# A two-pass state-space layer and a ConvLSTM on one core: PSUM banks, scan buffers and the slots of the preparation rearranged

## The chip, the cores and the metric

The kernel runs on one core of one Trainium2 chip. The metric is device time in microseconds (us), the median of several runs; lower is better.

## The reference, cut to what matters

The input has 64 channels, 256 time steps and 128 frequencies, in f32. Layer 0 runs a bidirectional Mamba block along time (128 sequences of length 256), then another along frequency (256 sequences of length 128), each with a forward and a backward direction. Layer 1 is a ConvLSTM, which the change doesn't touch. What counts here is the Mamba block:

```python
def _mamba(u, p):
    xz = jnp.einsum('nld,ed->nle', u, p['in_proj_w'])
    x, z = jnp.split(xz, 2, axis=-1)                      # 128 channels each
    x = silu(depthwise causal conv of 4 taps over x)
    dt, Bm, Cm = jnp.split(jnp.einsum('nld,ed->nle', x, p['x_proj_w']), [4, 20], axis=-1)
    dt = softplus(jnp.einsum('nlr,dr->nld', dt, p['dt_proj_w']) + p['dt_proj_b'])
    A = -jnp.exp(p['A_log'])                              # 128 channels x 16 states
    def step(h, inp):
        dt_t, B_t, C_t, x_t = inp
        h = jnp.exp(dt_t[:, :, None] * A) * h + dt_t[:, :, None] * B_t[:, None, :] * x_t[:, :, None]
        return (h, jnp.einsum('nds,ns->nd', h, C_t))
    y = scan(step) + x * p['Dp']
    return jnp.einsum('nld,od->nlo', y * silu(z), p['out_proj_w'])
```

The block normalises its input first (root mean square over channels) and adds the input at the end. So each pass has, for each direction, 128 channels x 16 states x 32768 positions of a first-order recurrence.

## The kernel before

`Stage` holds one pass; `tile_kernel` runs it twice, with L = 256 (time) and L = 128 (frequency). A pass goes over 64 chunks (NCH) of 512 positions (2 sequences of 256, or 4 of 128). A chunk has 16 steps S: 8 for each direction d. `where(S)` (L565) names a step by chunk, direction, q (which half of the states) and b (which 32 channels). One step handles 32 channels x 8 states x 512 positions, laid out as 128 partitions (4 groups j of states by 32 channels) x 1024 (two states g by 512 positions).

The work of one step:

- `inputs` (L570): 32 matmuls on PE put dt * x * B into a tile bx of two PSUM banks. The left operand is dtxT, dt * x transposed, 64 rows by 32 columns; the right one is D, a diagonal that carries B, 64 rows by 128 columns (L579).
- `decays` (L588): ACT computes exp(A * dt) into dA, a ring of 4 tiles, from rep, which is dt spread over the partitions (L599). The first column of each sequence is copied from zeros (L596), for the first four steps of each eight only, since the ring keeps it.
- `recur` (L601): one scan on VectorE, h <- dA, bx (L607), into one of 7 tiles h.
- `outputs` (L610): POOL multiplies h by C, spread over the partitions (L613).
- `add_up` (L615), once in four steps: 8 matmuls fold states and channels into y in PSUM (L622).

`skip` (L634), `gate` (L638), `close` (L642 on, po, L680) and `keep` (L686, L694) finish a direction or a chunk. D is built by `diagonal` on VectorE: mask, a tile in SBUF, times bt, which is B transposed and stands in a PSUM bank of its own (L471). It has 64 columns for each of two states; so a direction needs two of them (q = 0 and 1), each built in two halves: 8 instructions of 128 x 1024 a chunk.

The preparation of a chunk is done ahead, during the chunk before it. `run` (L711) writes the order out by hand, for every engine at once, step by step: scan S, gate, outputs of S - 1, add_up, inputs of S + 2, decays of S + 2 (two at once in the step of the silus, none in the next), and then whatever the table HEAD (L73) names for this slot. A slot is a step of the chunk before, from -12 (two chunks before) to 25. HEAD names load, squares, means, rms and normalise (slots -12 to -5), the projections of x and z (-2, -1, 0), the silus (6), the step sizes dt (6 and 7), dt_away (8 and 14: the step sizes written to a DRAM tensor named there, four copies), project_bc (8: B and C, and C written to a DRAM tensor named away), times_x (dtx, on POOL), turn (10 and 18: dtxT and bt by transposes on PE), spread_dt (rep read back from there) and spread_c (C read back from away). All DMAs are issued by SP, in this order. [...]

[...] two tiles bx of two banks (four banks), two banks `mm` that all projections, transposes and means take in turn, one for y, one for bt. A matmul into an `mm` bank waits until ACT has read what was there.

Of the kernel before, what the change touches and what calls it, by code (L numbers as in the profile page):

```python
# [29 lines left out]
F32 = mybir.dt.float32  # L30
BF16 = mybir.dt.bfloat16
AF = mybir.ActivationFunctionType
# [28 lines left out]
NRING = 4  # L61
NREP = 3
RESPOND = 12
NH = 7
LAG = 2
# [7 lines left out]
HEAD = (  # L73
    (-12, "load"),
    (-7.5, "squares"),
    (-6, "means"),
    (-6, "rms"),
    (-5, "normalise"),
    (-2, "project_x", 0),
    (-1, "project_z"),  # L80
    (0, "project_x", 1),
    (6, "silus"),
    (6, "step_sizes"),
    (7, "softplus"),
    (8, "dt_away", 0),
    (8, "project_bc", 0, 1),
    (8.5, "times_x", 0),
    (9.5, "spread_dt", 0, 0),
    (10, "turn", 0),
    (10, "spread_c", 0, 0),  # L90
    (11, "diagonal", 0, 0, 0),
    (12, "spread_dt", 0, 1),
    (12.5, "times_x", 1),
    (13, "diagonal", 0, 0, 1),
    (13.5, "spread_c", 0, 1),
    (14, "dt_away", 1),
    (15, "diagonal", 0, 1, 0),
    (17, "diagonal", 0, 1, 1),
    (17, "spread_dt", 1, 0),
    (17.5, "spread_c", 1, 0),  # L100
    (18, "turn", 1),
    (19, "diagonal", 1, 0, 0),
    (20, "spread_dt", 1, 1),
    (21, "diagonal", 1, 0, 1),
    (21.5, "spread_c", 1, 1),
    (23, "diagonal", 1, 1, 0),
    (25, "diagonal", 1, 1, 1),
)
SECOND = tuple(x for x in HEAD if x[0] >= 12 and x[1] != "dt_away")

# [114 lines left out]
class Stage:  # L225
# [8 lines left out]
    def __init__(self, ctx, m, stage, L, X, src, moments, gates):  # L234
# [5 lines left out]
        self.time = stage == 0  # L240
        n = f"s{stage}_"
        self.io = ctx.enter_context(tc.tile_pool(name=n + "io", bufs=1))
        self.wk = ctx.enter_context(tc.tile_pool(name=n + "wk", bufs=1))
        self.st = ctx.enter_context(tc.tile_pool(name=n + "st", bufs=NH))
        self.dram = ctx.enter_context(tc.tile_pool(name=n + "dram", bufs=3, space=bass.MemoryType.DRAM))
        fixed = ctx.enter_context(tc.tile_pool(name=n + "fixed", bufs=1))
        self.ps_mm = ctx.enter_context(tc.tile_pool(name=n + "mm", bufs=2, space=PSUM))
        self.ps_bx = ctx.enter_context(tc.tile_pool(name=n + "bx", bufs=2, space=PSUM))
        self.ps_y = ctx.enter_context(tc.tile_pool(name=n + "y", bufs=1, space=PSUM))
        self.ps_bt = ctx.enter_context(tc.tile_pool(name=n + "bt", bufs=1, space=PSUM))  # L250
# [4 lines left out]
        self.zeros = fixed.tile([P, 2, 2, self.nseq // 2, 1], F32, name="zeros", tag="zeros")  # L255
        nc.gpsimd.memset(self.zeros, 0.0)
        self.dA = []
        for k in range(NRING):
            self.dA.append(fixed.tile([P, 2, 2, self.nseq // 2, L], F32, name=f"dA{k}", tag=f"dA{k}"))
# [43 lines left out]
    def normalise(self, ch):  # L303
        nc, n, L, unp = self.nc, self.nseq // 2, self.L, self.unp
        xn = self.io.tile([P, n, L], F32, name="xn", tag="xn")
        nc.gpsimd.tensor_mul(xn, self.at["u", ch], self.rs)
# [24 lines left out]
    def gated(self, pz):  # L331
        for d in range(2):
            rows = slice(d * C, (d + 1) * C)
            self.nc.tensor.matmul(  # L334
                self.seqs(pz[d]),
                lhsT=self.m.Wz[self.stage][rows],
                rhs=self.unp[rows, :, 3 + d : 3 + d + self.L],
                start=True,
                stop=True,
            )  # L340

    def project_x(self, ch, d):
        i = 2 * self.stage + d
        px = self.mm("px")
        xs = self.wk.tile([P, NTOK], F32, name="xs", tag="xs", bufs=4)
        self.shifted(px, i)
        self.nc.scalar.activation(xs, px, AF.Identity, bias=self.m.cb[:, i : i + 1])  # L347
        self.at["xs", ch, d] = xs

    def project_z(self, ch):  # L350
        pz = [self.mm("pz") for _ in range(2)]
        self.gated(pz)
        for d in range(2):
            zs = self.wk.tile([P, NTOK], F32, name="zs", tag="zs", bufs=5)
            self.nc.scalar.copy(zs, pz[d])  # L355
            self.at["zs", ch, d] = zs
# [15 lines left out]
    def step_sizes(self, ch):  # L372
        for d in range(2):
            self.step_size(ch, d)

# [7 lines left out]
    def softplus(self, ch):  # L383
        self.nc.scalar.preload_act_table_set(SOFTPLUS)
        for d in range(2):
            self.soft(ch, d)
# [907 lines left out]
```

## Time and profile before

| what | us |
|---|---|
| median of 3 runs (7128.19 to 7153.43) | 7144.68 |
| the profiled execution | 7169.17 |
| its span | 7167.4 |
| busy: PE, VectorE (DVE), ACT, POOL | 5830.0, 6368.4, 4829.9, 5567.1 |
| VectorE idle ahead of its scans, in all | 497.4 |
| of that until PE's bx, until ACT's dA | 310.4, 157.8 |
| ACT idle until rep came by DMA | 163.7 |
| DMA: bytes moved, mean rate | 921.86 MB, 129 GB/s |

The profile is of one execution. A row of its groups gives line, engine, operation, output and inputs with their shapes, count, then the busy time in us and the mean of one in ns, then the time that the engine sat idle just before, and what ended that. In the timeline a row is one or several like instructions in order: start, duration, engine, line. PE's weight loads (PEld) run beside its matmuls. An f32 matmul shows as two records. Some 36 of 40 slices of the span belong to the two passes, the rest to the ConvLSTM.

### The profile page before, as it was taken

What the parts mean: (1) busy time and instruction counts of PE and PEld (TensorE: products, weight loads), DVE (VectorE), ACT (ScalarE), POOL (GpSimd) and SP (SyncE); (2) the same over time, 40 slices, a digit from 0 to 9 for tenths busy, and PEclk for the clock granted to TensorE, in tenths of its full rate; (3) what the DMA queues carried; (4) which work ended last, traced back from release to release, by engine and by line L of the source; (5) the groups of instructions that cost most, each with busy time, mean ns of one, the idle gap of its engine ahead of it and who ended that gap; (6) DMA issues with size and microseconds to landing.
All of it is one profiled execution on the core that took longest, in us unless ns stands there. A gap on an engine that the chain in (4) does not pass through costs nothing.

```text
span 7167.4 us, 327118 instructions
## 1 busy us (share of the span) xinstructions
PE 5830.0 (81%) x150024; PEld 3482.0 (49%) x150024; DVE 6368.4 (89%) x4166; ACT 4829.9 (67%) x8730; POOL 5567.1 (78%) x2898
## 2 busy tenths in 40 slices
PE   7878777777877787877888888787887878778998
PEld 4444444444444444444444444444444444447887
DVE  7999898889999999988988889999989899896887
ACT  6767676767767677767777677777767677763333
POOL 6888888778888888877887778888888788784554
PEclk9999999999999999999999899999999999999999
DMA  5555555555555555545555555555555555550000
GB/s 134 152 146 139 145 139 145 133 145 139 143 149 138 146 152 136 149 116 150 137 149 133 148 132 147 135 144 150 130 143 133 140 134 144 132 140 35 14 16 17
DMA packets 412666, 921.86 MB, mean 129 GB/s; under 512 B 52372, under 2 KB 142100, under 8 KB 411288
## 3 DMA queue, kind: packets, MB, share of 16 engines
q1 hardware_dynamic: 411288, 900.93, 48.8%
q8 instruction: 1177, 19.28, 1.1%
q14 instruction: 201, 1.65, 0.1%
HBM read 557.32 MB, written 310.38 MB: 121 GB/s over the span
## 4 chain that ended last, share of the span: by engine, by line
PE 25%; DVE 11%; ACT 8%; issue 6%; DMA 2%; POOL 2%; SPq 1%; DVEq 0%; POOLq 0%; ACTq 0%
DVE h L607 8%; PE bx L579 6%; PE cv L1048 6%; ACT dA L599 4%; PE y L622 3%; DVE D L471 2%; PE px L328 2%; PE px L329 1%; POOL h L613 1%; PE pv L370 1%; DMA unp<-xn 1%; PE pz L334 1%; PE pg L1104 1%; PE both L1160 1%; ACT L387 1%
## 5 line engine op out<-in xcount | busy, mean ns | idle before, releaser
L613 POOL TENSOR_TENSOR h<-h,C 128x1024 f32<-128x1024 f32 x2048 | 4826.7, 2374 | 974.8 <-DVE h L607 781.2
L607 DVE TENSOR_TENSOR_SCAN h<-dA,bx 128x1024 f32<-128x1024 f32 x2048 | 4618.0, 2276 | 497.4 <-PE bx L579 310.4
L579 PE MATMUL bx<-D,dtxT 64*32 64x128 f32 x131072 | 2509.0, 281 | 1180.5 <-DVE h L607 799.5
L579 PEld LDWEIGHTS bx<-D,dtxT 64*32 64x32 f32 x131072 | 1926.4, 108 | 2312.4 <-issue 1125.7
L599 ACT ACTIVATE dA<-rep,cols 128x510 f32<-128x510 f32 (+1 forms) x4096 | 2648.1, 710 | 171.2 <-DMA rep<-there 163.7
L471 DVE TENSOR_TENSOR D<-mask,bt 128x1024 f32<-128x1024 f32 x1026 | 1227.6, 1197 | 34.6 <-PE bt L458 34.0
L622 PE MATMUL y<-h,fold 128*32 128x512 f32 x8192 | 1106.4, 659 | 5.4 <-POOL h L613 5.4
L347 ACT ACTIVATE xs<-px,cols 128x512 f32<-128x512 f32 x252 | 173.4, 688 | 898.5 <-PE px L329 898.5
L622 PEld LDWEIGHTS y<-h,fold 128*32 128x32 f32 x8192 | 243.5, 117 | 612.8 <-issue 566.2
L407 POOL TENSOR_TENSOR dtx<-dt,xs 128x512 f32<-128x512 f32 x256 | 327.3, 1279 | 71.7 <-ACT dt L380 71.2
L460 ACT COPY dtxT<-pt 128x512 f32<-128x512 f32 x256 | 149.9, 585 | 300.6 <-PE pt L456 300.6
L328 PE MATMUL px<-unp,g 128*128 128x512 f32 x504 | 313.7, 706 | 46.5 <-DMA unp<-xn 46.3
L370 PE MATMUL pv<-xs,wdt 128*128 128x512 f32 x512 | 278.4, 669 | 34.0 <-ACT xs L364 31.8
L329 PE MATMUL px<-unp,g 128*128 128x512 f32 x504 | 277.3, 633 | 0.5 <-issue 0.5
L638 DVE TENSOR_TENSOR yz<-y,zs 128x512 f32<-128x512 f32 x256 | 172.7, 675 | 74.9 <-PE y L622 72.7
L355 ACT COPY zs<-pz 128x512 f32<-128x512 f32 x252 | 134.9, 586 | 154.5 <-PE pz L334 148.6
L1171 POOL TENSOR_TENSOR y<-v,X 128x512 f32<-128x512 f32 x32 | 40.6, 1269 | 231.2 <-DVE v L1169 231.2
L596 ACT COPY dA<-zeros 128x4 f32<-128x4 f32 (+1 forms) x1024 | 197.4, 193 | 5.4 <-DVE h L607 4.0
L634 ACT ACTIVATE y<-xs,cols 128x512 f32<-128x512 f32 x256 | 175.6, 686 | 9.5 <-DVE yz L638 9.5
L1120 ACT ACTIVATE a<-pg,cols,scale 128x488 f32<-128x488 f32 x128 | 86.5, 756 | 135.6 <-DVE pg L1118 135.6
L680 PE MATMUL po<-yz,w 128*64 128x256 f32 x1024 | 172.5, 400 | 0.9 <-ACT dA L599 0.9
L380 ACT ACTIVATE dt<-pv,cols 128x512 f32<-128x512 f32 x256 | 164.3, 684 | 12.7 <-issue 6.2
(190 smaller groups left out, 5195.8 us busy)
## 6 DMA issues: line engine op xcount, KB each, us to landing
there<-dt SPq DMA_DIRECT2D x1024, 256.0 KB
rep<-there SPq DMA_DIRECT2D x512, 512.0 KB
C<-away SPq DMA_DIRECT2D x512, 512.0 KB
away<-bc SPq DMA_DIRECT2D x1024, 32.0 KB
unp<-xn SPq DMA_DIRECT2D x504, 64.0 KB
u<-in_x SPq DMA_DIRECT2D x128, 64.0 KB
out<-y SPq DMA_DIRECT2D x32, 256.0 KB
w<-in_W_ih_f SPq DMA_DIRECT2D x10, 512.0 KB
```

The costliest lines, as they stand in the source:

```text
L328: nc.tensor.matmul(self.seqs(px), lhsT=m.G1[i], rhs=self.unp[:, :, first : first + L], start=True, stop=False)
L329: nc.tensor.matmul(self.seqs(px), lhsT=m.G2[i], rhs=self.unp[:, :, second : second + L], start=False, stop=True)
L370: self.nc.tensor.matmul(pv, lhsT=self.m.Wdt[i], rhs=self.at["xs", ch, d], start=True, stop=True)
L407: self.nc.gpsimd.tensor_mul(self.in_turns(dtx, own), self.in_turns(self.at["dt", ch, d], natural), self.in_turns(self.at["xs", ch, d], nat ...
L471: self.nc.vector.tensor_mul(D, self.m.mask.unsqueeze(1).unsqueeze(1).to_broadcast([P, n, 2, W]), b.unsqueeze(3).to_broadcast([P, n, 2, W]),)
L579: self.nc.tensor.matmul(bx[DB * j : DB * (j + 1), i, :, u], lhsT=dtxT[rows, u, DB * b : DB * (b + 1)], rhs=D[rows, u, j], start=True, stop ...
L596: nc.scalar.copy(dA[:, :, :, :, first : first + 1], self.zeros)
L599: nc.scalar.activation(dA[:, :, g, :, live], rep[:, :, :, live], AF.Exp, scale=m.A[:, k, n : n + 1])
L607: self.nc.vector.tensor_tensor_scan(h[:, step], dA[:, step], bx[:, step], 0.0, ALU.mult, ALU.add)
L613: self.nc.gpsimd.tensor_mul(h, h, self.at["C", ch, d, q])
L622: nc.tensor.matmul(y[DB * b : DB * (b + 1)].rearrange("p (i t) -> p i t", i=2), lhsT=self.m.fold, rhs=hs[b][:, g], start=False, stop=q == ...
L1048: self.nc.tensor.matmul(t[:, g, :, 0:n_out], lhsT=wts[s][:, gate * P : (gate + 1) * P], rhs=self.parts[n][:, :, s : s + n_out], start=s == ...
```

## The change

The change is in `Stage`, with a few lines in `Gates` and in the layout of the weights.

1. **PSUM.** bx gets three tiles (six banks). All projections, means, transposes and po share one bank `mm`. bt no longer has a bank: `turn_b` transposes B of both directions in that bank, and ACT copies it to a tile bT in SBUF, from which VectorE builds D.
2. **Scans over their decays.** dA is gone. ACT writes the decays into the tile h itself, the scan reads it and writes it in place. The first pass has 12 such tiles; the second has 7 of twice the width, each for two steps. Zeros are copied for every tile.
3. **Second pass.** A step takes 32 channels x 16 states x 256 positions, in place of 8 states x 512. D has 32 columns for each of four states, so one D serves a direction: 4 instructions a chunk. A matmul of bx takes 32 rows. `add_up` has 16 matmuls of 256 columns, in place of 8 of 512. rep comes in single tiles (`spread_one`), C as one tile for 16 states.
4. **Order.** bx is made 3 steps ahead (was 2), decays 4 (was 2), the gate comes a step later. The slots are new, and xn is made in the tile rs, in the second pass by VectorE (it was POOL). xs, zs, xn and the weights fetched for the second layer take less room.

The core of the diff:

```diff
+BOTH = (
+    (-8, "load"),
+    (-5, "squares"),
+    (-4, "means"),
+    (-4, "rms"),
+    (-3, "normalise"),
+    (1, "project_x", 0),
+    (2, "project_z", 0),
+    (4.5, "project_x", 1),
+    (5, "project_z", 1),
     (6, "silus"),
+    (6, "project_bc", 0, 1),
     (7, "softplus"),
     (8, "dt_away", 0),
     (8.5, "times_x", 0),
+    (8.5, "dt_away", 1),
+    (9.5, "turn_b"),
+    (10, "turn_x", 0),
+    (12.5, "times_x", 1),
+    (14, "turn_x", 1),
+)
+BY_Q = (
+    (9.5, "spread_two", 0, 0),
+    (10, "diagonal", 0, 0, 0),
+    (11, "spread_c", 0, 0),
+    (11.5, "spread_two", 0, 1),
+    (12, "diagonal", 0, 0, 1),
...
+    (24, "diagonal", 1, 1, 1),
+)
+BY_HALF = (
     (11, "diagonal", 0, 0, 0),
+    (11, "spread_c", 0, 0),
+    (12, "diagonal", 0, 0, 1),
+    (14, "diagonal", 1, 0, 0),
+    (15, "diagonal", 1, 0, 1),
+    (18, "spread_c", 1, 0),
 )
...
-        self.ps_mm = ctx.enter_context(tc.tile_pool(name=n + "mm", bufs=2, space=PSUM))
-        self.ps_bx = ctx.enter_context(tc.tile_pool(name=n + "bx", bufs=2, space=PSUM))
+        self.ps_mm = ctx.enter_context(tc.tile_pool(name=n + "mm", bufs=1, space=PSUM))
+        self.ps_bx = ctx.enter_context(tc.tile_pool(name=n + "bx", bufs=3, space=PSUM))
...
-        nc.gpsimd.tensor_mul(xn, self.at["u", ch], self.rs)
+        xn = self.rs
+        (nc.gpsimd if self.time else nc.vector).tensor_mul(xn, self.at["u", ch], xn)
...
     def softplus(self, ch):
         self.nc.scalar.preload_act_table_set(SOFTPLUS)
         for d in range(2):
+            self.step_size(ch, d)
             self.soft(ch, d)
...
+    def turn_b(self, ch, ds=(0, 1)):
+        bt = self.mm("bt")[:, 0 : NU * n].rearrange("p (u n) -> p u n", n=n)
...
+        nc.scalar.copy(
+            self.bT[:, ds[0] : ds[-1] + 1],
+            bt.rearrange("p u (d n) -> p d u n", n=NBC)[:, :, :, 0:NS],
+        )
...
+    def decay(self, S):
...
+        h = self.st.tile([P, 2, 2, L], F32, name="h", tag="h")
+        nc.scalar.copy(h.rearrange("p i g t -> p (i g) t")[:, :, first], self.zeros)
...
+            nc.scalar.activation(h[:, :, g, live], rep[:, :, live], AF.Exp, scale=m.A[:, d, n : n + 1])
...
+        self.nc.vector.tensor_tensor_scan(h, h, bx, 0.0, ALU.mult, ALU.add)
...
+    def ahead(self, S):
+
+        if self.time:
+            for n in (4, 5) if S % 16 == 6 else () if S % 16 == 7 else (4,):
+                if 0 <= S + n < 16 * NCH:
+                    self.decay(S + n)
+        elif S % 2 == 0 and 0 <= S + 4 < 16 * NCH:
+            self.decays(S // 2 + 2)
...
-            if 0 <= S + 2 < last:
-                self.inputs(S + 2)
-
-            for ahead in ((2, 3) if S % 16 == silu else () if S % 16 == silu + 1 else (2,)):
-                if 0 <= S + ahead < last:
-                    self.decays(S + ahead)
+            if 0 <= S + AHEAD < last:
+                self.inputs(S + AHEAD)
+            self.ahead(S)
             for f, args in steps.get(S, []):
                 f(*args)
```

`decays` in the second pass makes a tile of two steps at once (one copy of zeros, four activations). `ahead` stands before the slot's own entries, so of two things in one step the decays come first on ACT.

## The prediction

> **What bounds the kernel now.** I read the groups of instructions first, then the busy time by stage, then who waits for whom, then the timeline of one chunk.
>
> ```profile
> L613 POOL TENSOR_TENSOR h<-h,C 128x1024 f32<-128x1024 f32 x2048 | 4826.7, 2374 | 974.8 <-DVE h L607 781.2
> L607 DVE TENSOR_TENSOR_SCAN h<-dA,bx 128x1024 f32<-128x1024 f32 x2048 | 4618.0, 2276 | 497.4 <-PE bx L579 310.4
> ...
> L471 DVE TENSOR_TENSOR D<-mask,bt 128x1024 f32<-128x1024 f32 x1026 | 1227.6, 1197 | 34.6 <-PE bt L458 34.0
> ```
>
> The timeline gives scans from 45.5 to 3211.3 us in the first pass and from 3243.5 to 6473.5 in the second: 49.5 and 50.5 us for each of 64 chunks of 16 scans. Start to start a scan takes 2.2 us (two in 4.46 less 2.28), a D 1.1, a gate 0.6. So VectorE needs 16 x 2.2 + 8 x 1.1 + 2 x 0.6 = 45.2 us of a chunk. The busy time by stage says the same, here for a stretch of each pass (length, then PE, PEld, DVE, ACT, POOL, clock, DMA share, GB/s):
>
> ```profile
> 100.00:3200.00 3100.00, 2468.44 (x71765) 1388.03 (x71771) 2852.49 (x1630) 2215.89 (x3933) 2553.14 (x1189) 0.96 0.55 143
> 3300.00:6400.00 3100.00, 2512.29 (x70574) 1418.21 (x70576) 2797.71 (x1598) 2218.09 (x4079) 2508.90 (x1168) 0.93 0.55 140
> ```
>
> VectorE is busy 92% and 90%, so it sets the pace and 4 to 5 us of a chunk are waits. One chunk shows how much room the preparation of the next one has:
>
> ```profile
> 1607.05 4.46 DVE L607 TENSOR_TENSOR_SCAN h<-dA,bx 128x1024 f32<-128x1024 f32 x2
> ...
> 1641.24 2.29 DVE L607 TENSOR_TENSOR_SCAN h<-dA,bx 128x1024 f32<-128x1024 f32 x1
> ...
> 1614.34 1.28 ACT L360 ACT_TABLE_LOAD   x1
> ...
> 1635.43 1.33 ACT L599 ACTIVATE dA<-rep,cols 128x510 f32<-128x510 f32 x2 [1.54 <-DMA rep<-there]
> ...
> 1619.85 2.87 SPq L394 DMA_DIRECT2D there<-dt  x4
> 1624.24 5.75 SPq L442 DMA_DIRECT2D away<-bc  x8
> 1630.03 0.45 SPq L486 DMA_DIRECT2D rep<-there  x1
> ```
>
> The pair at 1607.05 is scans 4 and 5, the scan at 1641.24 is scan 16, the next chunk's first. Scan 4 ends at 1609.3. From there the silus begin 5.0 us later, the new step sizes come back spread as rep after 26.1, their decays are done after 27.6, and VectorE asks for them after 31.9. The slack is 4 us.
>
> [...]
>
> ```profile
> L471 DVE TENSOR_TENSOR D<-mask,bt x1026: 1193/1195/1223, 19.7 to 6456.9; 128x1024 f32<-128x1024 f32 x171
> ...
> L1126 DVE TENSOR_TENSOR c<-a x31: 1130/1140/1441, 6595.9 to 7147.5; 128x488 f32<-128x488 f32 x31
> ...
> L1127 DVE TENSOR_TENSOR c<-c,a x31: 666/667/669, 6597.1 to 7149.1; 128x488 f32<-128x488 f32 x31
> ...
> 6501.26 5.09 DVE L899 TENSOR_TENSOR acc<-acc,w 128x1024 f32<-128x1024 f32 x2
> ...
> 6499.65 5.62 POOL L899 TENSOR_TENSOR hi<-hi,w 128x1024 f32<-128x1024 f32 x2 [3.33 <-ACT w L896]
> ```
>
> D (minimum, median, maximum ns) reads bt from PSUM and never waits, though POOL is busy 82% of the time. L1126 reads two SBUF tiles while POOL is at L1125, and takes 473 ns more than L1127, its equal. At 6501 two such adds meet two of POOL's: they alternate, and each VectorE add keeps POOL out for about 1.07 us. [...]
>
> **The change, part by part.** Times below are us from the end of scan 4. PE's terms are start to start in the timeline of the chunk above (bx 1.1 a scan, px pair 1.95, pz 0.6, po 1.55, fold 1.85); ACT's are the durations of its rows there (table load 1.28, two decays 1.33, copies 0.5 to 0.6).
>
> *Fewer D.* In the second pass D goes from 8 to 4 a chunk: VectorE needs 40.8 us and 0.4 for xn. *D from SBUF.* bt is now copied by ACT to bT, so mask and bT are both SBUF[...]. POOL's chunk becomes, first pass, 16 x 2.33 (four in 9.36) + 2 x 1.23 (dtx) + 0.68 (xn) + 8 x 1.07 = 49.0; second 16 x 2.33 + 2.46 + 4 x 1.07 + 0.27 (xn, now VectorE's, 256 elements at D's rate) = 44.3. A D waits about 0.3 for POOL's rest in step with the scans. At best, then, the first pass stands where it is and the second falls to about 45.8 with 1.5 of left-over waits.
> *32-row tiles:* 32 matmuls a scan as before; I keep 1.1 us a scan. The bounds are a halving (0.55; half the rows) and double (2.2); PE, busy 80%, idles 0.6 us a scan and isn't the bound, so the low end gains nothing, and the high end would add 0.5 (1.1 less 0.6), 8 us a chunk. *Folds in the second pass:* 16 of 256 columns for 8 of 512, the same columns; from nothing to 8 x 0.117 (their weight loads), hidden while PE waits. *Scan over its decays:* same operands and 2.28 us; bounds 0 and a few ns[...]. *Zero copies:* 8 more a chunk in the first pass, 8 x 0.19 = 1.5 us of ACT, in the decays below. *Three banks, lookahead 3 and 4:* removes PE and ACT waits of (310 + 158)/128 = 3.7 us a chunk, if the preparation keeps up. What is late next is the preparation:
>
> *The slots and the single bank.* All projections now use one bank, each waiting for ACT's copy of the one before, with x and z moved from slots -2 to 0 to slots 1 to 5 and the silus left at 6. After scan 4, PE: bx 1.1, po 1.55, copy 0.5, px 1.95, fold 1.85, bx 1.1, pz 0.6, copy 0.6 = 9.2; then two decays at 1.45 ahead of the silus: they begin at 12.1, not 5.0. Table and silus 3.5, the two bc copies 1.2: 16.8. Queued behind on PE: bx 10 waits for the silus (pb stands ahead of it).
> Leg one, bT: table 1.3, softplus 0.65, then the second pv may only start once the bank is read (1.7 with its softplus), table 1.3, two decays 2.9, bT 0.3: 25. VectorE reaches D (slot 10) at about 16 to 19 and waits there, scans behind it. D 1.1, scans 11 to 15 at 2.2, two D at 1.4: scan 16 at 40, where VectorE alone needs 11 x 3.08 = 34.
> Leg two, rep: SP now has away (5.75) ahead of both dt_away, and the second dt_away, moved from slot 14 to 8.5, ahead of rep: 22.6. Behind it 2.1 MB of there, at 1.05 MB in 4.6 (full share) to 5.8 us (181 GB/s at 79% share in the first's 6 us): 10.4, u 0.6, rep 2.3 and 3.1 of latency (5.4 less 2.3 measured on rep): 39.0. Its decay 1.45: scan 16 at 40.5. Both legs agree.
> *rms behind it.* ACT has decay 16 (slot 12) ahead of rms, which POOL's xn waits for, with outputs 13 to 15 queued behind: rms 41.4, xn 0.7, three products 7.0, one D 1.1, fold 1.85, bx 1.1, px 1.95, bx 1.1, pz 0.6, bx twice 2.2 = 59, less bx 7's 1.1: the next scan 4 ends at 57.9 if all is in series. By VectorE (scans 16 to 20, two D, gate: 14.4) it is 54.9. I take the middle, 56.4.
> *Second pass:* no fold after scan 4, decay pairs of 2.7, rep in halves: T = 7.6 + 2.7 + 3.5 + 1.2 + 5.75 = 20.8; rep 7, there, rep 8 and latency 1.15 + 10.4 + 1.15 + 3.1: 36.6; decays 2.7, rms 0.9: 40.2. xn is VectorE's own here (slot 13), so scans 14 to 20 (15.4), xn 0.4, two D 2.3 and a gate 0.6 all come after: 58.9.
> *Sum:* 64 x (56.4 - 49.5) + 64 x (58.9 - 50.5) = 442 + 538 = 980. The profiled execution took 7169.2 (span 7167.4, 1.8 around it): 8149. The median shown is 24.5 below that execution: **8125**.
>
> **The rivals.** *Preparation hidden (faster).* If bT comes by 16 and rep by 30, only the sums with POOL stand: 50.3 (with 1.0 of waits) and 45.8, so 7169 + 64 x (0.8 - 4.7) = 6919, 6895 as a median. For it: lookahead is deeper by one scan and two decays. Against: the legs are 7 to 9 late, every term measured. It decides from 15 us less over a chunk of each pass (980/64). Chance 0.16.
> *Only the DMA leg is wrong.* With rep early the first pass still has leg one (54.4), the second ends at 48.7 (D 11 after bT at 23.0, scan 13 ended at 30): 7169 + 64 x (4.9 - 1.8) = 7367, 7343 as a median. For it: DMA's share is 0.55 on the whole.[...] Chance 0.17.
> *D loses its turn.* If POOL's next product always went first, each D would wait 2.33 more, 19 us a chunk in the first pass and 9 in the second: 7169 + 64 x 28 = 8961. The alternation at 6501 speaks against it; 0.03.
> *It doesn't do what it says:* the instruction order of the built kernel shows 4 D a chunk and bT in SBUF; no chance given.
>
> **Numbers.** The forecast's own range: down to 7645 if the first pass runs at VectorE's 54.9 (64 x 1.5) and both DMA legs are 3 us shorter (384), up to 8550, about the series reading (+96) and PE's issue waits in series as well (372 us on bx in the whole run, so 2.9 a chunk); 0.61. Rest, within 0.3% (about what a measurement can tell): 0.03. Slower 0.81, same 0.03, faster 0.16. The range reaches down to 7150, to take in the DMA rival and leave out the faster one.
>
> **What would show it.** Right: D waits for ACT's bT about 6 to 9 us a chunk in the first pass; in the second VectorE's xn waits for rms some 10 us; ACT's wait for rep over 250 us in all; D's longest duration well over 1223 ns, POOL's products with a tail near 3.4 us; PE's bx waiting less on scans. Wrong: D at 1195 throughout (no exclusion), or DVE's share at 90% or more (preparation hidden).

## The result, and the profile after

The changed kernel takes 8708.86 us (median of 4 runs, 8667.59 to 8715.72), the kernel before 7148.66 (7128.19 to 7153.43): a ratio of 1.218, 95% interval 1.213 to 1.222. It is slower, as forecast, but by 1560 us where 980 were forecast, and above the range (8550). The profiled execution took 8704.06, its span is 8702.2.

The scans run from 49.6 to 3899.0 us in the first pass and from 3940.2 to 8009.0 in the second, 60.1 and 63.6 us for each of 64 chunks, against 49.5 and 50.5 before. So 684 us of the difference lie in the first pass, 839 in the second. Below, a fill is the 32 matmuls (64 records) of one scan's bx, a fold the matmuls of one add_up, pb the projection of B and C, pv that of one direction's step sizes. The groups of the profile (busy us, mean ns | idle ahead):

```profile
L682 POOL TENSOR_TENSOR h<-h,C 128x1024 f32<-128x1024 f32 x2048 | 5274.4, 2602 | 674.0 <-DVE h L672 624.2
L672 DVE TENSOR_TENSOR_SCAN h<-h,bx 128x1024 f32<-128x1024 f32 x2048 | 4596.7, 2271 | 1224.0 <-PE bx L630 1161.4
...
L503 DVE TENSOR_TENSOR D<-mask,bT 128x1024 f32<-128x1024 f32 x512 | 1030.5, 2013 | 356.2 <-ACT bT L471 356.2
...
L503 DVE TENSOR_TENSOR D<-fold,bT 128x1024 f32<-128x1024 f32 x256 | 351.9, 1375 | 66.1 <-ACT bT L471 66.1
```

A scan costs what it did (2271 ns, 2276 before). D takes 2013 ns instead of 1197 in the first pass. Scans now wait 1161 us for fills (bx), 310 before. Busy time by stage (length, PE, PEld, DVE, ACT, POOL, clock, DMA share, GB/s):

```profile
100.00:3800.00 3700.00, 2768.45 (x69949) 1469.89 (x69940) 3184.00 (x1593) 2239.06 (x4411) 2793.40 (x1164) 0.88 0.48 118
3950.00:7950.00 4000.00, 3169.88 (x75384) 1840.62 (x75391) 2651.23 (x1433) 2282.16 (x4207) 2688.37 (x1124) 0.73 0.44 110
```

VectorE is busy 86% and 66%: it no longer sets the pace. (PE and PEld run beside each other: 2768 and 1470 us of the first stretch's 3700.) TensorE's granted clock has fallen from 0.96 and 0.93 to 0.88 and 0.73. VectorE's waits (total us, times, longest), in the first pass (66 to 3890) and then in the second (3945 to 7950):

```profile
DVE D L503 <- ACT bT L471: 353.8, 63, 6.3
DVE h L672 <- PE bx L630: 178.4, 72, 5.0
```

```profile
DVE h L672 <- PE bx L630: 969.9, 247, 7.3
DVE rs L314 <- ACT rs L309: 256.4, 62, 7.9
DVE h L672 <- POOL h L682: 61.0, 22, 2.8
DVE D L503 <- ACT bT L471: 54.7, 62, 2.6
```

With these the account of VectorE's time closes. First pass, a chunk: 45.2 of VectorE's own work (the prediction's sum), 8 D longer by 0.82 = 6.6, waits (353.8 + 178.4)/63 = 8.4: 60.2. Second: 40.8 + 0.4 for xn, 4 D longer by 0.18 = 0.7, waits 1342/63 = 21.3: 63.2. The account says where VectorE's time went. It doesn't say how much comes back when one part is taken away; the experiments do.

One chunk of each pass shows where the waits come from. First pass, VectorE and then ScalarE:

```profile
1628.95 2.27 DVE L672 TENSOR_TENSOR_SCAN h<-h,bx 128x1024 f32<-128x1024 f32 x1
...
1651.52 2.29 DVE L672 TENSOR_TENSOR_SCAN h<-h,bx 128x1024 f32<-128x1024 f32 x1 [3.64 <-PE bx L630]
1659.26 3.33 DVE L503 TENSOR_TENSOR D<-mask,bT 128x1024 f32<-128x1024 f32 x1 [5.45 <-ACT bT L471]
...
1675.01 4.45 DVE L672 TENSOR_TENSOR_SCAN h<-h,bx 128x1024 f32<-128x1024 f32 x2
...
1645.00 1.28 ACT L366 ACT_TABLE_LOAD   x1
...
1658.98 0.24 ACT L471 COPY bT<-bt 128x128 f32<-128x128 f32 x1
...
1674.93 1.33 ACT L652 ACTIVATE h<-rep,cols 128x510 f32<-128x510 f32 x2 [8.61 <-DMA rep<-there]
```

The scan at 1628.95 is scan 4; it ends at 1631.2. The silus' table is loaded 13.8 us later (12.1 forecast), bT is there 28.0 later (25), and D, with the scans behind it, waits 5.45. The pair at 1675.01 is scans 15 and 16, so scan 16 starts at 1677.2, 46 us after scan 4 (40 forecast). Its decays, which wait for rep, are done at 1676.3, 1 us before that. Second pass, TensorE, then VectorE:

```profile
5050.25 1.12 PE L341 MATMUL pz<-unp,wz 64*128 64x512 f32 x2
5051.30 1.15 PE L630 MATMUL bx<-D,dtxT 32*32 32x128 f32 x64
5056.53 2.44 PE L424 MATMUL pb<-xs,wbc 128*32 128x512 f32 x8 [4.08 <-ACT xs L370]
5058.91 1.96 PE L630 MATMUL bx<-D,dtxT 32*32 32x128 f32 x64
5060.80 2.08 PE L376 MATMUL pv<-xs,wdt 128*128 128x512 f32 x2
5063.65 2.08 PE L376 MATMUL pv<-xs,wdt 128*128 128x512 f32 x2 [0.78 <-ACT dt L382]
5065.66 3.09 PE L693 MATMUL y<-h,fold 128*32 128x256 f32 x32
5068.67 1.15 PE L630 MATMUL bx<-D,dtxT 32*32 32x128 f32 x64
...
5061.07 2.29 DVE L672 TENSOR_TENSOR_SCAN h<-h,bx 128x1024 f32<-128x1024 f32 x1 [6.13 <-PE bx L630]
5069.88 2.29 DVE L672 TENSOR_TENSOR_SCAN h<-h,bx 128x1024 f32<-128x1024 f32 x1 [6.53 <-PE bx L630]
```

TensorE stands idle for 4 us ahead of pb, which waits for the silus; the fill of scan 10 stands behind pb, that of scan 11 behind two pv and a fold. Scans 10 and 11 lose 12.7 us. The matmuls after the idle time are slow, too: the fill takes 1.96 instead of 1.15 us. The clock of this stretch (third from the end) in slices of 4 us:

```profile
5052.00:5056.00 4.00, 0.46 (x32) 0.19 (x15) 2.94 (x2) 3.97 (x7) 0.00 (x0) 0.80 0.00 0
5056.00:5060.00 4.00, 3.46 (x52) 1.47 (x58) 0.00 (x0) 2.99 (x6) 0.00 (x0) 0.50 0.01 4
5060.00:5064.00 4.00, 3.22 (x38) 1.26 (x20) 2.29 (x1) 2.18 (x3) 0.26 (x1) 0.50 0.13 24
5064.00:5068.00 4.00, 4.00 (x26) 1.34 (x29) 0.00 (x0) 2.21 (x4) 4.00 (x3) 0.50 0.40 104
5068.00:5072.00 4.00, 4.00 (x140) 2.32 (x133) 2.12 (x1) 2.42 (x4) 3.98 (x2) 0.99 0.91 257
```

### The profile page after: what moved, and what is told of

Same layout as the page of the kernel before. It is cut to its first block, busy times and chain, and to the rows that moved or that the text cites. A ratio compares the mean times of both kernels' runs of the same rounds, so it can differ in the third digit from the quotient of the medians.

```text
span 8702.2 us, 334895 instructions
## 1 busy us (share of the span) xinstructions
PE 6817.5 (78%) x153616; PEld 4009.1 (46%) x153616; DVE 6577.1 (76%) x3971; ACT 4922.9 (57%) x9372; POOL 6021.9 (69%) x2835
## 4 chain that ended last, share of the span: by engine, by line
PE 29%; ACT 11%; DVE 4%; DMA 4%; SPq 4%; issue 2%; POOL 0%; POOLq 0%; DVEq 0%; ACTq 0%
PE bx L630 8%; ACT h L664 6%; PE cv L1133 5%; PE y L693 5%; DVE h L672 3%; DMA rep<-there 3%; SPq L397 3%; PE pv L376 2%; PE px L336 2%; PE pb L424 2%; PE px L337 1%; PE pz L341 1%; ACT L366 1%; DVE D L503 1%; SPq L458 1%
## 5 line engine op out<-in xcount | busy, mean ns | idle before, releaser
L682 POOL TENSOR_TENSOR h<-h,C 128x1024 f32<-128x1024 f32 x2048 | 5274.4, 2602 | 674.0 <-DVE h L672 624.2
L672 DVE TENSOR_TENSOR_SCAN h<-h,bx 128x1024 f32<-128x1024 f32 x2048 | 4596.7, 2271 | 1224.0 <-PE bx L630 1161.4
L630 PE MATMUL bx<-D,dtxT 64*32 64x128 f32 (+1 forms) x131072 | 2881.2, 314 | 945.9 <-DVE h L672 732.7
L630 PEld LDWEIGHTS bx<-D,dtxT 64*32 64x32 f32 (+1 forms) x131072 | 2209.7, 119 | 2188.2 <-issue 1052.5
L652 ACT ACTIVATE h<-rep,cols 128x510 f32<-128x510 f32 x2048 | 1358.8, 714 | 442.1 <-DMA rep<-there 441.7
L664 ACT ACTIVATE h<-rep,cols 128x508 f32<-128x508 f32 x2048 | 1303.6, 709 | 355.0 <-DMA rep<-there 353.9
L693 PE MATMUL y<-h,fold 128*32 128x256 f32 (+1 forms) x12288 | 1267.1, 526 | 97.6 <-POOL h L682 96.8
L503 DVE TENSOR_TENSOR D<-mask,bT 128x1024 f32<-128x1024 f32 x512 | 1030.5, 2013 | 356.2 <-ACT bT L471 356.2
L424 PE MATMUL pb<-xs,wbc 128*32 128x512 f32 x1024 | 313.1, 1044 | 524.7 <-ACT xs L370 518.8
L503 DVE TENSOR_TENSOR D<-fold,bT 128x1024 f32<-128x1024 f32 x256 | 351.9, 1375 | 66.1 <-ACT bT L471 66.1
```

The costliest lines, as they stand in the source:

```text
L424: nc.tensor.matmul(pb[first : first + NBC], lhsT=self.m.Wbc[:, 2 * self.stage + d, n], rhs=self.at["xs", ch, d], start=True, stop=True,)
L503: nc.vector.tensor_mul(self.at["D", ch, d, q].rearrange("p u j s c -> p (u j) s c")[:, own], mask.unsqueeze(1).unsqueeze(1).to_broadcast(s ...
L630: self.nc.tensor.matmul(bx[DB * j : DB * (j + 1), i, :, u], lhsT=dtxT[rows, u, DB * b : DB * (b + 1)], rhs=D[rows, u, j], start=True, stop ...
L652: nc.scalar.activation(h[:, :, g, live], rep[:, :, live], AF.Exp, scale=m.A[:, d, n : n + 1])
L664: nc.scalar.activation(h[:, :, s, live], rep[:, :, live], AF.Exp, scale=m.A[:, 2 + d, n : n + 1])
L672: self.nc.vector.tensor_tensor_scan(h, h, bx, 0.0, ALU.mult, ALU.add)
```

## The experiments

Medians; a ratio is to the kernel before, run beside it on the same chip (7128 to 7136 us; 7149 for the changed kernel). The last two columns are us a chunk in each pass, from first to last scan in the trace, over 64.

| run | us | ratio (95%) | pass 1 | pass 2 |
|---|---|---|---|---|
| before | 7148.66 | | 49.5 | 50.5 |
| changed | 8708.86 | 1.218 (1.213 to 1.222) | 60.1 | 63.6 |
| *one part of the change in the kernel before* | | | | |
| e1 D from SBUF | 7268.98 | 1.020 (1.017 to 1.022) | 50.3 | 50.9 |
| e10 late x and z slots | 7927.81 | 1.111 (1.109 to 1.114) | 56.0 | 55.7 |
| e11 one projection bank | 7496.94 | 1.050 (1.046 to 1.054) | 51.8 | 52.5 |
| e14 order of pb and SP | 7590.78 | 1.064 (1.061 to 1.066) | 53.1 | 53.5 |
| e16 e10, e11 and e14 together | 8387.80 | 1.175 (1.172 to 1.178) | 59.2 | 59.9 |
| *taken away from the changed kernel* | | | | |
| e2 single bank (and third fill bank) | 8825.28 | 1.238 (1.235 to 1.241) | 62.0 | 63.7 |
| e3 the same, and D from SBUF | 8767.23 | 1.230 (1.227 to 1.234) | 62.7 | 62.0 |
| e4 x and z behind the closing products | 8674.72 | 1.219 (1.215 to 1.223) | 60.0 | 63.1 |
| e5 late rms | 8667.14 | 1.214 (1.212 to 1.217) | 60.2 | 62.6 |
| e6 C and second dt ahead of rep | 8731.93 | 1.224 (1.222 to 1.226) | 60.7 | 63.6 |
| e7 both of these | 8640.90 | 1.212 (1.209 to 1.214) | 59.5 | 63.1 |
| e8 idle time ahead of pb | 8638.25 | 1.211 (1.209 to 1.213) | 59.6 | 63.1 |
| e9 most late slots | 8402.71 | 1.177 (1.173 to 1.180) | 57.5 | 61.9 |
| e12 these, banks and D from SBUF | 8275.28 | 1.160 (1.156 to 1.163) | 57.9 | 59.5 |
| e13 e12, and SP's order | 7955.92 | 1.114 (1.111 to 1.118) | 53.2 | 59.2 |
| e15 the whole new preparation | 8018.61 | 1.124 (1.121 to 1.126) | 53.7 | 59.6 |
| e17 e15, TensorE kept busy | 8015.86 | 1.124 (1.122 to 1.126) | 54.7 | 58.8 |
| e18 e15, D apart | 7904.79 | 1.108 (1.106 to 1.109) | 53.7 | 57.8 |

Of e4 to e8 none is more than 0.8% from the changed kernel, and only e8's interval lies, barely, outside the changed kernel's; their gains and losses are at the edge of what these runs can tell.

The first theory was the prediction's: a longer preparation (late slots, single bank, rep's way) together with the longer D (2013 ns in the mean of the first pass, 1197 before), which the texts below call the exclusion, or D's turns. Its rivals were any one of these alone.

### e1: D from SBUF, alone

```diff
+        nc.scalar.copy(bT, bt)
...
-        self.at["dtxT", ch, d], self.at["bt", ch, d] = t, bt
+        self.at["dtxT", ch, d], self.at["bt", ch, d] = t, bT
```

> The kernel before, with one part of the change: B turned is copied by ScalarE from PSUM to SBUF, and D reads that copy; everything else as before. Theory of the exclusion: each D meets POOL's products and takes 2.0 us in the mean instead of 1.2, as in the changed kernel's first pass, 8 x 0.8 = 6.5 us of VectorE a chunk, of which the 4 to 5 us of waits before can absorb about 1 to 2: 4.5 to 6.5 x 128 chunks = +580 to +830 us, near 7730 to 7980. Rival (D's turn is taken out of waits that exist anyway, and the late preparation alone made the change slow): within 100 us of before.

Measured: +140 us, between the two, and much nearer to the rival's. D's durations (minimum, median, maximum ns), its group in the profile, and then the first pass's busy time in this run:

```profile
L473 DVE TENSOR_TENSOR D<-mask,bT x1026: 1191/1430/3451, 20.2 to 6539.3; 128x1024 f32<-128x1024 f32 x171
```

```profile
L473 DVE TENSOR_TENSOR D<-mask,bT 128x1024 f32<-128x1024 f32 x1026 | 1756.6, 1712 | 24.9 <-ACT bT L460 24.3
```

```profile
100.00:3200.00 3100.00, 2407.15 (x70687) 1357.52 (x70691) 3056.09 (x1604) 2200.33 (x4007) 2924.89 (x1172) 0.96 0.53 141
```

D is longer with this edit alone: up to 3.45 us and 1712 ns in the mean, 515 more than before, though less than the changed kernel's 2013. But VectorE is now busy 98.6% of the time instead of 92%: what D takes more has come in the place of waits that stood there before. Of some 4.1 us a chunk (8 x 0.515), 0.9 reach the end in the first pass and 0.4 in the second.

### e2, e3: the banks dealt out again, without and with D from PSUM

```diff
-        self.ps_mm = ... name=n + "mm", bufs=1
-        self.ps_bx = ... name=n + "bx", bufs=3
+        self.ps_mm = ... name=n + "mm", bufs=3     (e3: bufs=2, and a bank for bt)
+        self.ps_bx = ... name=n + "bx", bufs=2
...
-AHEAD = 3
+AHEAD = 2
```

In e3 D reads bt in PSUM and direction one is turned at slot 17.5 (first pass) or 13.

> The changed kernel with its banks dealt differently: three banks for projections instead of one, two double banks for the fills instead of three, so fills run 2 scans ahead instead of 3. Theory of the late preparation with the single bank as its cause: px, pz, po, pb and both pv no longer wait for ScalarE's copies, 3 to 5 us a chunk: about 8200 to 8350. If the slots set it and not the bank: within 100 us of 8709. If the third fill bank was worth something: slower than 8709. The exclusion theory expects D's mean unchanged at 2.0 us in the first pass.

> The changed kernel with B turned kept in a PSUM bank of its own, which D reads; two banks for projections, two double ones for the fills, the turn of direction one back at slot 17.5 or 13. Beside the run with three projection banks this takes away the exclusion and ScalarE's copy. Exclusion theory: D's longest is 1.22 us again, first pass 5 to 6.5 us a chunk shorter than in that run, second 1 us: 350 to 480 us less than it. Rival (the exclusion costs nothing, since VectorE waits anyway): within 100 us of that run.

Measured: 8825 and 8767, 116 and 58 us above the changed kernel. The theory of the single bank falls as the sole cause; a fill less ahead costs at least as much as the banks give. In e3 D takes 1.22 us at most, yet the run is only 58 us below e2 (350 to 480 expected), and the first pass is no shorter: with D's turns gone, VectorE just waits longer for other things. That is the rival's case again.

### e4: x and z of direction one ahead of the closing products

```diff
-    (4.5, "project_x", 1),
-    (5, "project_z", 1),
-    (6, "silus"),
+    (4, "project_x", 1),
+    (4, "project_z", 1),
+    (5.5, "silus"),
```

> The changed kernel with three slots changed: x and z of direction one at slot 4, before the closing products, instead of 4.5 and 5 behind them; the silus at 5.5, ahead of the decays of slot 6. Banks and D as changed. Theory of the late preparation: the silus begin 4 to 6 us earlier after scan 4, and as VectorE waits for what follows them in both passes, a chunk is 3 to 5 us shorter: 8709 - 128 x 3 to 5 = 8070 to 8330. Rival (rep's way through SP sets it): within 100 us of 8709.

Measured: -34, the rival's, but inconclusive, since the edit brought a cost of its own. The silus do begin sooner, 11.5 us after scan 4 in one chunk (13.8), but the decays now lie between them and B's copy, and force one more table load:

```profile
1642.87 1.28 ACT L652 ACT_TABLE_LOAD   x1
...
1646.72 0.56 ACT L434 COPY bc<-pb 64x512 f32<-64x512 f32 x1
```

### e5, e6, e7: the way of rep

e5 puts the slots of the load to the normalise back to -12, -7.5, -6, -6, -5. e6 reorders SP:

```diff
     (8, "dt_away", 0),
-    (8.5, "dt_away", 1),
+    (10, "go_away"),            # C's 8 writes, no longer in project_bc
+    (14, "dt_away", 1),
```

> The changed kernel with the slots of the load, the squares, the means, rms and the normalise as they were before (-12, -7.5, -6, -6, -5 for -8, -5, -4, -4, -3): rms then stands on ScalarE ahead of the decay that waits for the next chunk's first rep, and the normalised input no longer waits for that transfer. Theory of the ring: the first rep of a chunk releases rms, rms the normalised input, that the x projection, the silus, the step sizes and so the next rep, and this closed ring of about 60 us sets both passes; cut at rms, the chunk falls to what scans and the way from scan 4 to rep need, 55 of 60.1 and 56 of 63.9: about 128 x 5 to 6.5 less, near 7900 to 8070. Rival (rms has time, the ring closes elsewhere, through scan 4 and PE's queue): within 100 us of 8709.

> The changed kernel with another order on SP: the first direction's step sizes go away, rep is fetched, only then C goes away (slot 10), and the second direction's step sizes leave at slot 14, as before the change. Rms, banks and D as changed. Theory of the ring: 8 writes of C (5.75 us), 4 of step sizes (3 us and 1 MB) stand no longer ahead of rep, so rep comes about 10 us earlier and the ring is as much shorter until the way of B turned takes over: a chunk is 5 to 8 us shorter, near 7700 to 8070. Rival (rep is not in what sets the time): within 100 us of 8709; if C comes too late for POOL instead, slower.

> Both edits of the two runs beside it: rms early and rep ahead of C and of the second step sizes. Theory of the ring: what is left is the way of B turned, with VectorE's own work longer by D's turns: 54 and 49 us a chunk in the sums, near 7300 to 7600. If the gains of the two are the same gain, no better than the better of them.

Measured: -42, +23 and -68. e5 and e6 are the rivals' cases; e7 is far from the 7300 to 7600 of its theory. ScalarE's waits for rep were 796 us in the changed kernel. In e6 (second pass, then first, and then two of VectorE's waits, for fills and for rms):

```profile
ACT h L671 <- DMA rep<-there: 92.9, 67, 4.6
...
ACT h L659 <- DMA rep<-there: 0.7, 1, 0.7
```

```profile
DVE h L679 <- PE bx L637: 1538.6, 424, 7.4
...
DVE rs L315 <- ACT rs L310: 52.0, 48, 14.2
```

700 us of ScalarE's waiting are gone, and not one from the time. VectorE's wait for rms fell with them, from 271 to 52 us, and its waits for fills rose from 1161 to 1539. So rep, and rms behind it, were late, but they did not set the changed kernel's pace alone: the fills were as late. The theory of a ring through rep falls.

### e8: TensorE kept busy ahead of pb

```diff
         pb = self.mm("pb")
+        if len(ds) == 2:
+            for _ in range(6):
+                nc.tensor.matmul(pb, lhsT=self.m.ident, rhs=..., start=True, stop=True)
```

> The changed kernel with six more matmuls of 512 columns (about 3.6 us) in pb's bank ahead of pb's own, which overwrite their result: they run while TensorE would wait about 4 us for the silus of every chunk, and keep it busy. Theory of the clock: after that idle time TensorE runs at half its clock through pb, the two pv and the folds of the second pass (pv 0.94 us instead of 0.68); kept busy, the granted clock of the second pass rises from 0.73 towards 0.9 and its chunk falls by 3 to 5 us: 8709 - 64 x 3 to 5 = 8390 to 8520. Rival (the slow clock costs only time that the ring has to spare): within 60 us of 8709 at the higher clock.

```profile
100.00:3800.00 3700.00, 3002.67 (x71320) 1569.39 (x71315) 3203.12 (x1606) 2259.25 (x4452) 2816.07 (x1174) 0.91 0.48 118
3950.00:7900.00 3950.00, 3204.76 (x75932) 1868.39 (x75932) 2626.24 (x1435) 2265.68 (x4184) 2711.74 (x1123) 0.81 0.45 112
```

The clock rises from 0.88 and 0.73 to 0.91 and 0.81; the time falls by 71 us, 0.5 a chunk, near the rival's. The clock of 0.50 after this wait is not the main cause. With 0.81 in the mean, other slow stretches stayed.

### e10, e11, e14, e16: parts of the preparation in the kernel before

```diff
-    (-2, "project_x", 0),
-    (-1, "project_z"),
-    (0, "project_x", 1),
+    (1, "project_x", 0),                # e10, e16
+    (2, "project_z", 0),
+    (4.5, "project_x", 1),
+    (5, "project_z", 1),
...
-        self.ps_mm = ... name=n + "mm", bufs=2
+        self.ps_mm = ... name=n + "mm", bufs=1     # e11, e16
...
     (6, "silus"),
+    (6, "project_bc", 0, 1),            # e14, e16
     (6, "step_sizes"),
...
-    (8, "project_bc", 0, 1),
+    (8.5, "dt_away", 1),
-    (14, "dt_away", 1),
```

With one bank each step size's matmul stands by its softplus.

> The kernel before with one part of the change: x and z are projected at slots 1, 2, 4.5 and 5, one z at a time, as in the changed kernel; its two projection banks, two fill banks, D from PSUM, SP's order, rms and the slots from 6 on stay. Theory of the stretch: that alone pushes the silus 7 us back behind scan 4 and makes fills wait behind what needs them: +5 to +9 us a chunk, 7131 + 128 x 5 to 9 = 7770 to 8280. Rival (it takes the single bank or the order of pb and pv too): within 200 us of before.

> The kernel before with another part of the change alone: one projection bank instead of two, so each z by itself at slot -1, and each step size's matmul by its softplus in slot 7; the x and z slots stay before slot 1, D from PSUM, two fill banks. Theory of the stretch: the chain has slack of several slots there, each wait for a copy costs 0.5 to 1 us of TensorE, 2 to 4 a chunk, part of it hidden: +0 to +350, 7130 to 7480. Theory of the single bank as the cause: +700 or more.

> The kernel before with the order of the preparation as changed, alone: pb with its 8 writes of C at slot 6 ahead of the step sizes instead of slot 8 behind them, the second direction's step sizes away at slot 8.5 instead of 14. x and z slots, banks, D as before. Theory of two limits: rep comes some 8 to 10 us later, and had about 4 us to spare: +3 to +6 us a chunk, 7520 to 7900. Rival (hidden): within 100 us of before.

> The kernel before with three parts of the change together: late x and z slots, one projection bank, and the new order of pb, step sizes and second step sizes. Tiling, D from PSUM, two fill banks as before. Theory: these are what made the change slow in both passes: 58 to 63 us a chunk, 8200 to 8800, about the changed kernel's 8709. If the parts hide one another: not far above 7930, the late slots alone.

Measured: +792, +362, +455, and +1252 for the three together (their sum would be 1609). All four fall within what the longer preparation expects, or just above it (e11), and all three parts count. e14 moves both pb and the second step sizes; what each of the two costs was not separated. In e10 it is again the fills behind the preparation that VectorE waits for (310 us before):

```profile
DVE h L610 <- PE bx L582: 990.7, 435, 6.4
```

In the first pass e16's 59.2 and the 0.9 that e1 adds come to the changed kernel's 60.1. That is a sum of two runs and not a run, and e15 below finds another price in that pass, so it doesn't show that nothing else counts there. In the second pass 3.3 of 13.1 us are left over.

### e9, e12, e13: late slots taken away, then what showed behind them

```diff
-    (1, "project_x", 0),
-    (2, "project_z", 0),
-    (4.5, "project_x", 1),
-    (5, "project_z", 1),
+    (-2, "project_x", 0),
+    (-1, "project_z", 0),
+    (0, "project_z", 1),
+    (3.5, "project_x", 1),
```

with rms early as in e5 and more zs tiles (the gate writes over zs for that). e12 adds e3's edits, e13 also e6's.

> The changed kernel with x of direction zero and both z back at slots -2, -1 and 0, x of direction one at 3.5, ahead of the closing products, rms and the load at their earlier slots; the gate writes over zs, which pays for the two further zs tiles. One projection bank, three fill banks, D from SBUF, SP's order as changed. Theory of the stretch: with everything from px to the silus between slots 1 and 6, TensorE's order puts fills 10 and 11 and the turn of B behind a chain of turns between TensorE and ScalarE that runs 28 to 33 us from the first px to the second pv, while scans 4 to 9 fill 15 of it; starting from slot 3.5 with one px left, the chain is some 10 us shorter, and 8 to 12 us of waits a chunk (5.5 for B and 2.8 for fills in the first pass, 12.6 and more for fills in the second) go: 8709 - 128 x 8 to 10 = 7430 to 7690. Rivals (single bank, rep, D's turns): within 150 us of 8667, the run with rms early.

> The edits of the early run and of the run with D from PSUM together: early x and z, rms early, two projection banks, two fill banks, B turned in a PSUM bank of its own; what is left of the change is the second pass's 16 states per slot with 4 D a chunk, scans over their decays, decays four slots ahead, pb ahead of the step sizes and SP's order. Theory of the stretch: better than the early run by D's turns, 5 us a chunk in the first pass: 7000 to 7350. Rival: what is left (pb first, SP's order) keeps it above 7500.

> The early run with D from PSUM, and SP's order changed too: step sizes of direction zero and rep go first, C after them (slot 10), the second direction's step sizes at slot 14. Theory of two limits side by side: in the early run the normalised input and rep come late (TensorE waits 300 us for it in the first pass, 5 us a chunk; ScalarE up to 9 us for rep), which C and the second step sizes ahead of them cause; with both legs cut the first pass falls from 57.7 to about 50 a chunk and the second by 3 to 5: 8275 - 64 x 7.5 - 64 x 4 = 7540, 7400 to 7700. Rival (SP's order gives nothing, as in the run with rep first alone): within 100 us of 8275.

Measured: -306, -434 and -753, each less than expected. In e12 the x projection waits for the normalised input, which SP sends behind 8 writes of C and 8 of the step sizes; e13's order takes that away. e12, then e13:

```profile
PE px L339 <- DMA unp<-rs: 340.2, 74, 8.2
```

```profile
PE px L340 <- DMA unp<-rs: 14.4, 16, 3.7
```

The first pass falls from 57.9 to 53.2. The same edit gave nothing in e6. That is two limits side by side: SP's order counts only once the late slots, the single bank and D's turns are gone. The second pass does not move (59.5, 59.2), against the 3 to 5 us expected.

### e15, e17, e18: the old preparation with the new scans

e15 gives the changed kernel the preparation of before (slots, banks, order, D from PSUM); left are 16 states per slot, scans over their decays, decays four ahead. For room it also writes the gate over zs and rms over the squares, which the changed kernel doesn't. e17 adds matmuls of constants ahead of those that overwrite them; e18 has D at slots 11, 13, 20, 21 for 11, 12, 19, 20 in the second pass, and xn on POOL.

```diff
+    (3, "busy_po"),                     # e17
+    (11, "busy_pt", 10),
+    (12, "busy_pt", 6),
...
-    (12, "diagonal", 0, 0, 1),          # e18
+    (13, "diagonal", 0, 0, 1),
```

> The changed kernel with the whole preparation as it was before: x and z at -2 to 0, rms early, step sizes ahead of pb, second step sizes at 14, two projection banks, two fill banks, B turned in PSUM, D at the slots of before. What is left of the change: 16 states per slot and 4 D a chunk in the second pass, scans over their decays, decays four slots ahead; the gate writes over zs and rms over the squares, for room. Theory of the preparation: the first pass is as before (49.5), the second 4 D of 1.1 us shorter and a wait or two better, 45.5 to 48: 7131 - 64 x 2.5 to 5 = 6810 to 6980. Rival (the new tiling costs TensorE or the order of scans something of its own): above 7150.

> The changed kernel with the old preparation, and matmuls of constants (256 columns, about 0.3 us each) ahead of those that overwrite them: 10 before the first step size, 8 at slot 3 in the closing products' bank, 10 and 6 at slots 11 and 12 in the bank of the second turn of x. Theory of the clock: granted clock from 0.83 to 0.92 or more, fills at 1.15 us again, second pass from 59.9 to about 53, first from 53.8 to 51: 8018 - 64 x 7 - 64 x 3 = 7400, 7250 to 7650. Rival (the clock is only a companion, TensorE's order and rep set the waits): the clock rises and the time stays within 100 us of 8018, or grows by part of the 10 us a chunk that is added.

> The changed kernel with the old preparation, and in the second pass the normalise on GpSimd as it was before, D at slots 11 and 13, 20 and 21 instead of 11 and 12, 19 and 20: between two scans VectorE has one thing less to do, so TensorE waits 3.6 us less at one place. Theory of the clock: one of three slow stretches of a chunk, the longest of 17 us, goes or is shorter, 2 to 5 us a chunk in the second pass: 7700 to 7890. Rival (VectorE's order doesn't matter): within 80 us of 8018.

Measured: 8019, 883 above the kernel before, where the theory had 6810 to 6980. The rival holds: what is left of the change (the scan side, below) has a price of its own, 4.2 us a chunk in the first pass and 9.1 in the second. e13, with quite another preparation, comes to the same 53.2 and 59.2. VectorE waits for fills, 431 us in the first pass and 1064 in the second, where it was 310 in all before (66 to 3460, then 3540 to 7300 us):

```profile
DVE h L670 <- PE bx L628: 431.1, 260, 4.2
```

```profile
DVE h L670 <- PE bx L628: 1063.6, 477, 6.0
```

A stretch of e15's second pass, first one fill, then slices of 2 us, with TensorE's busy time first after the length and the clock third from the end:

```profile
5012.02 1.96 PE L628 MATMUL bx<-D,dtxT 32*32 32x128 f32 x64 [3.60 <-DVE h L670]
```

```profile
5010.00:5012.00 2.00, 0.00 (x0) 0.02 (x1) 2.00 (x2) 0.00 (x0) 0.80 (x1) 0.60 0.94 289
5012.00:5014.00 2.00, 1.96 (x64) 1.52 (x64) 2.00 (x2) 1.59 (x3) 1.99 (x1) 0.50 0.99 221
...
5022.00:5024.00 2.00, 2.00 (x19) 1.25 (x6) 2.00 (x2) 0.97 (x2) 0.65 (x1) 0.50 0.64 207
5024.00:5026.00 2.00, 2.00 (x4) 0.67 (x2) 1.45 (x1) 0.12 (x1) 2.00 (x2) 0.50 0.24 86
...
5028.00:5030.00 2.00, 2.00 (x37) 0.79 (x25) 1.66 (x1) 0.74 (x4) 0.02 (x1) 1.00 1.06 266
```

VectorE does the gate, D and xn ahead of a scan, and TensorE idles for 3.6 us until that scan frees a bank. By the slices its clock then stands at 0.50 for about 17 us, in which TensorE waits twice more and works through the last 8. e17 lifts the clock from 0.74 to 0.94 in the second pass, and the time stays. That does not clear the clock: the added matmuls took 17 us of TensorE a chunk in its trace (10 were expected), such as

```profile
5000.46 4.58 PE L382 MATMUL pt<-wbc,ident 128*128 128x256 f32 x20
...
5032.00 5.41 PE L382 MATMUL po<-wbc,ident 128*128 128x256 f32 x16
```

so gain and cost can't be told apart. e18 gains 114 us, 1.8 a chunk in the second pass, somewhat under the 2 to 5 expected: VectorE's D and xn in a row are a part of the price, not most of it. None of these versions beats the kernel before.

## Why the prediction was wrong

The direction was right. In the first pass the mechanism was right and its terms were too small; in the second the chain that the prediction followed was not the one that set the pace. That is the step that failed.

- **Second pass: rep, rms, xn.** This step failed. The prediction ran the chunk through "rep 7, there, rep 8 and latency", the decays, rms and xn to 58.9, and put what fills cost at nothing ("PE ... isn't the bound"). rep was late, but xn's wait for rms came to 4.1 a chunk, not 10, and when e6 took most of it away the pass stayed at 63.6. In its place stand 15.4 a chunk of waits for fills (969.9/63): scans 10 and 11 wait for fills that stand in TensorE's order behind pb, both pv and a fold. The prediction had noted that fill 10 waits for the silus, without a term for it in this pass. That these fills set the pace is read from the trace; no run moved pb and pv behind them alone. That the forecast of 58.9 came near 63.6 was luck: the chain that it followed was not the one at work.
- **First pass: both legs, too short.** bT came 28.0 us after scan 4 (25 forecast); D's wait is 5.6 a chunk (6 to 9). From D at slot 10 to the start of scan 16 the chunk takes 17.9 (1659.3 to 1677.2), where the prediction has 15: 2.5 of the difference is longer D, and the rest is the gate, which its sum left out. So scan 16 starts at 46, not 40. rep's leg was nearly as much too short: its decays were done at 45.0, not 40.5. That rep comes behind all that SP issues ahead of it was the prediction's assumption; e6, with C and the second step sizes behind rep, brought ScalarE's waits for it from 796 us to 94. "Both legs agree" came true within 1 us; either one is then enough, which fits e6. From scan 16 on the forecast holds. This chunk takes 61.5; the mean, 60.1, is 3.7 above the 56.4 that the prediction took as a middle.
- **D from SBUF.** A longer D was forecast and came, but not by so much: "A D waits about 0.3" for POOL; the mean is 0.82 more than before in the first pass (0.18 in the second). The first D of the chunk above, begun at 1659.26 while a product of POOL ran to 1661.50, took 3.33 us. With bt in PSUM the longest D took 1.22 us (before, e12), with bT in SBUF 3.36 and 3.45 (changed, e1); that D then waits for POOL is the author's reading of such overlaps. The 0.82 is 6.6 a chunk where 2.4 were counted. No run shows that taking it away gives as much back: alone it costs 0.9 a chunk or less (e1), and without it e3's first pass was no shorter than e2's.
- **TensorE's durations.** All its terms were taken from a trace with the clock at 0.96 and 0.93. In the second pass, behind a wait of 4.08 us, they ran at a clock of 0.50: a pv 2.08 us in the chunk above (its mean record was 712 ns in the second pass, now it is 944). TensorE's busy time a chunk went from 40.9 to 50.4 in the second pass. e8 lifts the clock there from 0.73 to 0.81 and gains 0.5 a chunk, so what it took away is a small term; the slow stretches that stayed were not priced.
- **The new scan side.** "From nothing to 8 x 0.117" for the folds and "bounds 0 and a few ns" for the scans over their decays: with the preparation of before, what is left of the change comes with 4.2 and 9.1 us a chunk more (e15). The parts hide one another: 9.7 and 9.4 by the preparation (e16), 4.2 and 9.1 by the scan side, 10.7 and 13.1 together.

Most of the prediction's signs came true: D's wait for bT (5.6, a little under), rep's waits (796 us for "over 250"), D's longest 3361 ns (1223 before), POOL's longest 3397 (2412). They show that the waits are there, and a chain can be late as forecast without being the one that decides. (By the lines shown, the decays before the change were done after 27.4 us, not 27.6; nothing rests on it.)

What stays open is how e15's price divides. It shows as waits for fills. VectorE waits for decays for only 37 us in all, so the late rep (943 us of ScalarE's waits over both passes, 164 before) can count only through what ScalarE does next. One such way shows in the trace: pv, with fills behind it, waits 310 us for the silus (32 before). Why the fills come late there was not separated further: the pairs of folds stand in two successive slots beside the projections, the clock is 0.74 in the second pass, the first pass has no new tiling at all and is slower too, and the edits for room were never tried alone; only VectorE's D and xn were moved apart. In e2 the gain of the banks and the loss of a fill ahead were not separated.

## What to carry to other kernels

A wait in the profile is not a limit: 700 us of waits went without moving the time, since another chain, as late, stood beside it. When two chains are late, price each of them for the case that the other is mended, and follow every engine's queue in order: here the fill of scan 10 stood behind a pb that waited 4.08 us for ScalarE, and the scan waited 6.13 for the fill. And if a change makes an engine idle, don't carry its durations over from a trace in which it was kept busy: the mean record of pv went from 712 to 944 ns.

## What was unexpected of the hardware

After a wait of 3.6 us (e15, above) and one of 4.1 (the changed kernel, ahead of pb) TensorE's granted clock is 0.50. An estimate from the slices, if the clock stood at 1.00 until it fell, puts the fall 2 us after the start of each of the two: 0.80 over 5052 to 5056 means 0.50 in the last 1.6 us, and the wait began at 5052.4; e15's 0.60 over 5010 to 5012 gives the same. Another wait, of 4.46 us from 1660.4 on in the changed kernel's first pass, shows 1.00 until 1664 and 0.74 from 1664 to 1666, so 2 us is no rule. The clock stays at 0.50 for about 14 us in the changed kernel and 17 in e15, with TensorE busy in the last 8 of them but for one wait of 0.78. In the changed kernel's first pass, after a like wait ahead of pb (4.16 us), it was back after 7 (0.62 over 1644 to 1646, 0.50 to 1650, 0.67 to 1652, then 1.00); what makes the difference no run here shows. In the changed kernel a fill of 32 rows takes 1.15 us at a clock of 1.00 (at 5051.30) where one of 64 rows takes 1.16 (at 1657.16), and either takes 1.96 at 0.50 (at 5058.91 and 1649.36): the prediction was right to keep 1.1 us for it.
